# A two-layer graph kernel: the gate with tokens stationary and 256 weight columns moving, c brought to tokens through DRAM, one pool of eight PSUM banks, every order from a table

## The chip, the cores and the metric

The kernel runs on one core of a Trainium2 chip. The metric is the time of one execution on the device, in microseconds. A core has five engines with a queue of instructions each: TensorE (PE, matmuls into PSUM), VectorE (DVE), ScalarE (ACT), GpSimd (POOL) and SyncE (SP), which here issues all DMAs. An instruction starts when those ahead of it on its engine have started and the semaphores that it waits for have been reached, so the order on each engine is part of the kernel. PSUM has eight banks of 128 x 512 fp32.

## The reference

64 graphs of N = 256 tokens with H = 512 features, all fp32, and an adjacency `adj` of 256 x 256 per graph. Cut to what is computed:

```python
h = relu(layernorm(x))
q, k, v = h @ Wq.T, h @ Wk.T, h @ Wv.T               # 8 heads of 64
s = where(adj != 0, q @ k.T / 8, -inf)               # per head
c = softmax(s) @ v
gate = sigmoid(concat([c, h]) @ Wg.T + bg)
x = x + gate * h + (1 - gate) * c
h = relu(layernorm(x))
wh = h @ W
e = leaky_relu(wh @ a1 + (wh @ a2).T, 0.2)
x = x + elu(softmax(where(adj == 0, -1e9, e)) @ wh)
```

## The kernel before

Per graph there are four large products, q and k together, v, the gate's z and wh, each of 256 tokens by 512 by 512 (z by 1024). They use a Strassen-like scheme of seven products of halves (`strassen`, L163). The products 1, 2, 3 and so on accumulate in three PSUM banks a, b and c (matmuls at L179); ACT copies bank a out (L192: u1 and quadrant c00) and DVE adds banks b and c to earlier sums (L190: u2, u3, c11, c10, c01). Sums of the weights are made once on DVE; sums of the tokens' operand for every product on POOL (`token_sums`, L157 to L160; tile S).

Layer 0. x is loaded, normalised (bn on DVE L201 to L205, power on POOL L209, relu on ACT L218), transposed as 32 x 32 blocks on DVE (L261) and completed by a trip through DRAM: four sends, four fetches (`send_blocks`, `fetch_blocks`). hT then is channel-major. Scores (L360) of the eight heads take 16 matmuls in two halves; DVE finds each row's maximum with the mask (L375), ACT takes exp with its sum (L384), DVE the reciprocal (L392), POOL (three quarters, L399) or ACT scales, DVE transposes blocks (L408), and the attention weights go through DRAM to become eT (one send and four fetches a quarter). `a_weigh` (L440) multiplies them with v into pc, which ACT copies to cT, channel-major (L450).

The gate, `g_gate`, uses `on_channels` (L316): a 128 x 128 block of the weight is stationary and 128 token columns move, so that z is channel-major. tanh (L483) takes bg per channel as its bias. POOL makes d = hT - cT (L478); DVE makes d = (z + 1) d (mix 1, L491) and z = d / 2 + cT (mix 2, L493), which is y, transposes its blocks (L509), and y comes to tokens through DRAM (`g_send`, `g_fetch`); `g_residual` (L531) adds it to x on DVE. The last two graphs transpose y on PE (L504).

Layer 1 normalises x again and brings h1 through DRAM; wh has two extra columns, from which come the logits (pe, a transpose on PE, L586). The softmax's weights eg go through DRAM to egT. `g_out` (L645) has four matmuls of 512 columns a graph into two banks po. DVE takes neg = min(po r, 0) (L658), ACT pos = relu(po r) (L663) and exp of neg (L664), DVE adds (elu, L669), POOL adds to x (L674), and x is stored.

PSUM: banks ma, mb and mc serve the products and two or three of the scores, pool w with five banks all else. `emit_round(i)` (L698) writes out the order of all engines for one round by hand: PE does pc, scores, po, z, wh, qk with pe in it, and v, of four graphs at different stages (p = i + 1, q = i - 1, r = i - 2, o = i - 3). `emit_end` writes out the last rounds. Graphs below FIRST = 3 and from LAST = 62 on are transposed on PE.

Of the kernel before, what the change touches and what calls it, by code (L numbers as in the profile page):

```python
# [20 lines left out]

@with_exitstack
def kernel(
# [13 lines left out]

# [9 lines left out]
    FIRST, LAST = 3, B - 2  # L65
    assert N == 256 and H == 512 and SCALE == 0.125

    def pool(name, bufs, **kw):
# [3 lines left out]
    st = pool("st", 3)  # L72
    sb = {tag: pool(tag, bufs) for tag, bufs in {
        "x": 5, "adj": 1, "mask": 4, "hT": 3, "S": 3, "qk": 2, "v": 2, "wh": 1, "e": 5,
        "cT": 1, "z": 2, "h": 1, "tmp": 5, "U": 3,
    }.items()}
    ps = {tag: pool(f"ps_{tag}", bufs, space=bass.MemoryType.PSUM) for tag, bufs in {
        "ma": 1, "mb": 1, "mc": 1, "w": 5,
    }.items()}
    dram = pool("dram", 4, space=bass.MemoryType.DRAM)  # L80

# [3 lines left out]
    nc.gpsimd.memset(mhalf, -0.5)  # L85

    graphs = {}

    def load_graph(g):
        xt = sb["x"].tile([P, NT, H], F32, tag="t", name=f"x_{g}")  # L90
        at = sb["adj"].tile([P, NT, N], I32, tag="t", name=f"adj_{g}")
        for ts in [slice(0, NT)] if g > 0 else [slice(t, t + 1) for t in range(NT)]:
            nc.sync.dma_start(xt[:, ts, :], x[g].rearrange("(t p) h -> p t h", p=P)[:, ts, :])
        graphs[g] = {"x": xt, "adj": at}
        if g > 0:
            load_edges(g)

    def load_edges(g):
        nc.sync.dma_start(graphs[g]["adj"], adj[g].rearrange("(t p) n -> p t n", p=P))
# [4 lines left out]
    def load_weight(key, eng):  # L104
        w = weight[key] = const.tile([P, HC, 2, HH + (key == "1")], F32, name=f"w{key}_sb")
        for n in range(2):
            eng.dma_start(w[:, :, n, :HH], sources[key][:, n * HH:(n + 1) * HH].rearrange("(c p) f -> p c f", p=P))

    def weight_sums(key):

        w = weight[key]
        t = const.tile([P, 3, 2, w.shape[3]], F32, name=f"w{key}_t")
        b11, b12, b21, b22 = (w[:, r:r + 2, n, :] for r in (0, 2) for n in range(2))
        weight[key] = {1: b11, 2: b21, 3: b22, 4: t[:, 2], 5: b12, 6: t[:, 0], 7: t[:, 1]}
        return [lambda args=args: nc.vector.tensor_tensor(*args) for args in (
            (t[:, 1], b22, b12, ALU.subtract),
            (t[:, 0], t[:, 1], b11, ALU.add),
            (b12, b12, b11, ALU.subtract),
            (t[:, 2], b21, t[:, 0], ALU.subtract),
        )]  # L120

    a_sb = [sb["tmp"].tile([P, H], F32, tag="t", name=f"a_sb_{side}") for side in range(2)]
    hbg = const.tile([P, HC], F32, name="hbg")

    def load_small():
        for side in range(2):
            nc.sync.dma_start(a_sb[side], bass.AP(tensor=a.tensor, offset=a.offset + side * H, ap=[[0, P], [1, H]]))
        with nc.allow_non_contiguous_dma(reason="512 biases, once"):
            nc.sync.dma_start(hbg, bg.rearrange("(c p) -> p c", p=P))

    def edge_columns():

        w = weight["1"]

        def column(c, side):
            scr = sb["tmp"].tile([P, 2, HH], F32, tag="t", name=f"scr_{c}_{side}")
            nc.vector.scalar_tensor_tensor(
                scr, w[:, c, :, :HH], 1.0, a_sb[side].rearrange("p (n f) -> p n f", n=2),
                ALU.mult, ALU.mult, accum_out=w[:, c, side, HH:],
            )  # L140

        return [lambda c=c, side=side: column(c, side) for c in range(HC) for side in range(2)]

    def evac(dst, src, on_act):
        if on_act:
            nc.scalar.copy(dst, src)
        else:
            nc.vector.tensor_copy(dst, src)


    def token_sums(hT, name):

        s = sb["S"].tile([P, 4, 2, P], F32, tag="t", name=f"S_{name}")
        a11, a21 = hT[:, 0, 0:2, :], hT[:, 1, 0:2, :]
        a12, a22 = hT[:, 0, 2:4, :], hT[:, 1, 2:4, :]
        eng = nc.gpsimd
        eng.tensor_tensor(s[:, 0], a21, a22, ALU.add)  # L157
        eng.tensor_tensor(s[:, 1], s[:, 0], a11, ALU.subtract)
        eng.tensor_tensor(s[:, 2], a11, a21, ALU.subtract)
        eng.tensor_tensor(s[:, 3], a12, s[:, 1], ALU.subtract)  # L160
        return {1: a11, 2: a12, 3: s[:, 3], 4: a22, 5: s[:, 0], 6: s[:, 1], 7: s[:, 2]}

    def strassen(name, shape, mms, dst):  # L163

        bank, u = {}, {}
        where = {"1": "a", "2": "a", "6": "b", "7": "b", "4": "b", "5": "c", "3": "c"}
        sums = {"u2": ("b", "u1"), "u3": ("b", "u1"), "c11": ("c", "u3"), "c10": ("b", "u1"), "c01": ("c", "u2")}  # L170

        def run(step):
            if step in where:
                key, first, last = where[step], step in "165", step in "243"
                if first:
                    bank[key] = ps[f"m{key}"].tile(shape, F32, tag="t", name=f"pm{key}_{name}")
                todo = mms(int(step))
                for i, (cols, lhsT, rhs) in enumerate(todo):
                    nc.tensor.matmul(  # L179
                        bank[key][(slice(None), *cols)], lhsT, rhs,  # L180
                        start=first and i == 0, stop=last and i == len(todo) - 1, skip_group_check=True,
                    )
                return
            if step[0] == "u":
                out = u[step] = sb["U"].tile(shape, F32, tag="t", name=f"{step}_{name}")
            else:
                out = dst[int(step[1])][int(step[2])]
            if step in sums:
                key, other = sums[step]
                nc.vector.tensor_tensor(out, bank[key], u[other], ALU.add)  # L190
            else:
                nc.scalar.copy(out, bank["a"])  # L192

        return run

    def norm_stats(s, t, name):

        if t == 0:
            s["mv"] = st.tile([P, NT, 2], F32, tag="mv", name=f"mv_{name}")
        bs = st.tile([P, 6], F32, tag="bs", name=f"bs_{name}_{t}")  # L200
        nc.vector.bn_stats(bs, s["x"][:, t, :])  # L201
        nc.vector.bn_aggr(s["mv"][:, t, :], bs)
        if t == NT - 1:
            s["ve"] = st.tile([P, NT], F32, tag="ve", name=f"ve_{name}")
            nc.vector.tensor_scalar_add(s["ve"], s["mv"][:, :, 1], EPS)  # L205

    def norm_root(s, name):
        s["rs"] = st.tile([P, NT], F32, tag="rs", name=f"rs_{name}")
        nc.gpsimd.tensor_tensor(s["rs"], s["ve"], mhalf, ALU.pow)  # L209

    def norm_bias(s, name):
        s["nb"] = st.tile([P, NT], F32, tag="nb", name=f"nb_{name}")
        nc.vector.scalar_tensor_tensor(s["nb"], s["mv"][:, :, 0], -1.0, s["rs"], ALU.mult, ALU.mult)  # L213

    def norm_relu(s, name):
        h = sb["h"].tile([P, NT, H], F32, tag="t", name=f"h_{name}")
        for t in range(NT):
            nc.scalar.activation(  # L218
                h[:, t, :], s["x"][:, t, :], AF.Relu, bias=s["nb"][:, t:t + 1], scale=s["rs"][:, t:t + 1]
            )  # L220
        return h


    def p_mask(g):
        s = graphs[g]
        s["mask"] = sb["mask"].tile([P, NT, N], BF16, tag="t", name=f"mask_{g}")
        nc.vector.tensor_scalar(s["mask"], s["adj"], 0.0, MASKED, ALU.is_equal, ALU.mult)

    def p_stats(g, t):
        norm_stats(graphs[g], t, f"l0_{g}")  # L230

    def p_root(g):
        norm_root(graphs[g], f"l0_{g}")

    def p_bias(g):
        norm_bias(graphs[g], f"l0_{g}")

    def p_norm(g):
        graphs[g]["h"] = norm_relu(graphs[g], f"l0_{g}")

    def p_first():

        s = graphs[0]
        s["h"] = sb["h"].tile([P, NT, H], F32, tag="t", name="h_l0_0")
        mv, ve, rs, nb = (
            st.tile([P, NT, n], F32, tag=tag, name=f"{tag}_l0_0") for tag, n in (("mv", 2), ("ve", 1), ("rs", 1), ("nb", 1))
        )
        for t in range(NT):
            bs = st.tile([P, 6], F32, tag="bs", name=f"bs_l0_0_{t}")
# [4 lines left out]
        for t in range(NT):  # L254
            nc.vector.scalar_tensor_tensor(nb[:, t, :], mv[:, t, :1], -1.0, rs[:, t, :], ALU.mult, ALU.mult)
            nc.scalar.activation(s["h"][:, t, :], s["x"][:, t, :], AF.Relu, bias=nb[:, t, :], scale=rs[:, t, :])
# [790 lines left out]
```

## Time and profile before

| | us |
|---|---|
| three runs | 3148.56 to 3149.49, median 3148.71 |
| profiled execution, span from first to last instruction | 3150.9 |
| first matmul of qk, graphs 0, 1 and 2 | 9.2, 39.5, 88.0 |
| first matmul of po of the last graph | 3140.2 |

The profiled execution's own time is not listed beside its span; the span lies 2.2 us above the median of the runs. The granted clock is 0.999 in the mean. Queue 1 moved 585 MB in 1.1 million packets and took 74.8% of the 16 DMA engines. In profile rows a group such as `pmb_z<-S_c,wgc_t` names the output and the inputs as tiles; times are in us, the mean of one instruction in ns, and behind the second bar stand the idle time before the group and what ended it.

### The profile page before, as it was taken

What the parts mean: (1) busy time and instruction counts of PE and PEld (TensorE: products, weight loads), DVE (VectorE), ACT (ScalarE), POOL (GpSimd) and SP (SyncE); (2) the same over time, 40 slices, a digit from 0 to 9 for tenths busy, and PEclk for the clock granted to TensorE, in tenths of its full rate; (3) what the DMA queues carried; (4) which work ended last, traced back from release to release, by engine and by line L of the source; (5) the groups of instructions that cost most, each with busy time, mean ns of one, the idle gap of its engine ahead of it and who ended that gap; (6) DMA issues with size and microseconds to landing.
All of it is one profiled execution on the core that took longest, in us unless ns stands there. A gap on an engine that the chain in (4) does not pass through costs nothing.

```text
span 3150.9 us, 66781 instructions
## 1 busy us (share of the span) xinstructions
PE 3118.2 (99%) x22768; PEld 2726.6 (87%) x22768; DVE 2486.6 (79%) x6373; ACT 1419.0 (45%) x3977; POOL 1524.0 (48%) x2178
## 2 busy tenths in 40 slices
PE   8999999999999999999999999999999999999998
PEld 7888988888889889888888888888988988889886
DVE  7787787877877877878778778787787787877876
ACT  3354453453544544435435445354454453543543
POOL 3354454544544545545445455454454554544543
PEclk9999999999999999999999999999999999999999
DMA  5777878778777777787787777877878778778772
GB/s 171 188 184 182 202 182 196 194 184 203 185 182 203 188 192 196 179 205 188 178 210 183 188 189 183 203 186 181 206 185 194 192 181 205 187 179 209 184 178 81
DMA packets 1098180, 589.60 MB, mean 187 GB/s; under 512 B 681584, under 2 KB 1024112, under 8 KB 1097840
## 3 DMA queue, kind: packets, MB, share of 16 engines
q1 hardware_dynamic: 1097840, 585.32, 74.8%
q8 instruction: 183, 3.00, 0.4%
q14 instruction: 157, 1.29, 0.1%
HBM read 304.35 MB, written 280.76 MB: 186 GB/s over the span
## 4 chain that ended last, share of the span: by engine, by line
PE 94%; DVE 2%; DMA 2%; SPq 1%; ACT 0%; issue 0%; POOL 0%; DVEq 0%; ACTq 0%
PE pmb_z L179 11%; PE pmb_qk L179 10%; PE pma_z L179 7%; PE po L645 7%; PE pmc_z L179 7%; PE ps L360 7%; PE pma_qk L179 7%; PE pmc_qk L179 7%; PE pc L440 7%; PE pmb_wh L179 5%; PE pmb_v L179 5%; PE pmc_wh L179 3%; PE pma_wh L179 3%; PE pmc_v L179 3%; PE pma_v L179 3%; DMA eT<-there_e 1%
## 5 line engine op out<-in xcount | busy, mean ns | idle before, releaser
L384 ACT ACTIVATE e<-e,low 128x256 f32<-128x256 f32 x1024 | 508.3, 502 | 65.8 <-DVE low L375 64.9
L209 POOL TENSOR_TENSOR rs_l<-ve_l,mhalf 128x2 f32<-128x2 f32 x127 | 88.5, 697 | 882.3 <-DVE ve_l L205 882.3
L375 DVE CUSTOM_DVE_ANT_0 e<-ps,mask 128x256 f32<-128x256 f32 x1024 | 362.1, 415 | 102.7 <-PE ps L360 102.7
L399 POOL TENSOR_SCALAR e<-e,rec 128x256 f32<-128x256 f32 x768 | 354.6, 480 | 149.9 <-DVE rec L392 101.8
L408 DVE STREAM_TRANSPOSE eb<-e 128x512 f32<-128x512 f32 x512 | 351.6, 696 | 78.5 <-POOL e L399 65.4
L674 POOL TENSOR_TENSOR x<-x,pos 128x512 f32<-128x512 f32 x122 | 152.7, 1273 | 285.7 <-DVE pos L669 285.7
L218 ACT ACTIVATE h_l<-x,nb_l,rs_l 128x512 f32<-128x512 f32 x254 | 193.1, 808 | 214.9 <-DVE nb_l L213 134.8
L440 PE MATMUL pc<-eT,v 128*64 128x256 f32 x2048 | 239.5, 384 | 7.7 <-DMA eT<-there_e 6.9
L360 PE MATMUL ps<-qk 64*128 64x256 f32 x2048 | 239.0, 383 | 0.9 <-DVE qk L190 0.9
L645 PE MATMUL po<-wh,egT 128*128 128x512 f32 x512 | 237.0, 605 | 0.7 <-ACT egT L628 0.7
L360 PEld LDWEIGHTS ps<-qk 64*128 64x128 f32 x2048 | 193.4, 187 | 45.2 <-DVE ve_l L205 20.0
L157 POOL TENSOR_TENSOR S_l<-hT_l 128x256 f32<-128x256 f32 x128 | 95.6, 747 | 275.0 <-DMA hT_l<-there_h 242.6
L440 PEld LDWEIGHTS pc<-eT,v 128*64 128x64 f32 x2048 | 141.9, 137 | 97.2 <-issue 17.6
L261 DVE STREAM_TRANSPOSE h_l<-h_l 128x512 f32<-128x512 f32 x246 | 166.6, 696 | 54.8 <-ACT h_l L218 54.8
L384 ACT ACTIVATION_READ_ACCUMULATOR e<-e,low 128x1 f32 x1024 | 197.6, 193 | 0.0
L645 PEld LDWEIGHTS po<-wh,egT 128*128 128x128 f32 x512 | 92.2, 190 | 113.2 <-issue 92.0
L201 DVE BATCH_NORM_STATS2 bs_l<-x 128x6 f32<-128x512 f32 x254 | 171.6, 676 | 0.1
L483 ACT ACTIVATE z<-z,hbg 128x256 f32<-128x256 f32 x256 | 116.5, 504 | 105.8 <-DVE z L190 105.8
L450 ACT COPY cT<-pc 128x512 f32<-128x512 f32 x128 | 74.9, 586 | 190.7 <-PE pc L440 190.7
L478 POOL TENSOR_TENSOR d<-hT_l,cT 128x512 f32<-128x512 f32 x128 | 160.7, 1275 | 0.0
L179 PEld LDWEIGHTS pma_z<-hT_l,wgh_sb 128*128 128x128 f32 x1024 | 130.0, 193 | 29.6 <-issue 29.6
L192 ACT COPY qk<-pma_qk 128x512 f32<-128x512 f32 x64 | 37.5, 586 | 236.2 <-PE pma_qk L179 236.2
(157 smaller groups left out, 8115.6 us busy)
## 6 DMA issues: line engine op xcount, KB each, us to landing
there_e<-eb SPq DMA_DIRECT2D x256, 512.0 KB, 4.0
eT<-there_e SPq DMA_DIRECT2D x1024, 128.0 KB, 4.1
there_h<-h_l SPq DMA_DIRECT2D x492, 128.0 KB, 3.3
hT_l<-there_h SPq DMA_DIRECT2D x492, 128.0 KB, 3.2
x<-in_x_dram SPq DMA_DIRECT2D x63, 512.0 KB, 3.9
out_dram<-x SPq DMA_DIRECT2D x63, 512.0 KB, 4.6
there_y<-y SPq DMA_DIRECT2D x62, 512.0 KB, 3.0
yT<-there_y SPq DMA_DIRECT2D x248, 128.0 KB, 3.7
```

Of the source, the lines that this page charges most:

```text
L179: nc.tensor.matmul(bank[key][(slice(None), *cols)], lhsT, rhs, start=first and i == 0, stop=last and i == len(todo) - 1, skip_group_check= ...
L201: nc.vector.bn_stats(bs, s["x"][:, t, :])
L218: nc.scalar.activation(h[:, t, :], s["x"][:, t, :], AF.Relu, bias=s["nb"][:, t:t + 1], scale=s["rs"][:, t:t + 1])
L261: nc.vector.transpose(h[:, t, :], h[:, t, :])
L360: nc.tensor.matmul(psc[jj, i][:, t, :], qk[r:r + DK, 0, jj, t * P:(t + 1) * P], qk[r:r + DK, 1, jj, :], start=True, stop=True,)
L375: nc.vector.tensor_tensor_reduce(s["e", half, jj][:, i, t, :], s["ps", half][jj, i][:, t, :], s["mask"][:, t, :], -SCALE, HUGE, ALU.add, A ...
L384: nc.scalar.activation(e, e, AF.Exp, bias=s["low", half][:, jj, i, t:t + 1], scale=-1.0, accum_out=s["sums", half][:, jj, i, t:t + 1],)
L399: nc.gpsimd.tensor_scalar(e, e, rec[:, i, t:t + 1], 1.0, ALU.mult, ALU.mult)
L408: nc.vector.transpose(s["eb", half, jj][:, :, 4 * i:4 * i + 4, :].rearrange("p b n c -> p n b c"), e)
L440: nc.tensor.matmul(pc[i * DK:(i + 1) * DK, jj, :].rearrange("p (t a c) -> p t a c", t=NT, c=32), s["v"][:, kc, hd * DK:(hd + 1) * DK], eT[ ...
L478: nc.gpsimd.tensor_tensor(d, s["hT"][:, :, js, :], s["cT"][:, :, js, :], ALU.subtract)
L645: nc.tensor.matmul(pm, s["egT"][:, t, kc, :], s["wh"][kc][:, :, :HH], start=(kc == 0), stop=(kc == NT - 1))
```

## The change

The kernel is rewritten as named steps. A table (`PLAN`) gives each step of a graph a key; graph g's keys are shifted by 48 g, and the instructions of all engines are written in the order of the sorted keys. The keys order the work and hold no instruction back. Graphs 0, 1, 2, 61, 62 and 63 have tables of their own (`MOVED`), the weights and what is done once another. What changes in the work:

- z is computed with tokens stationary and 256 weight columns moving, as v and wh already were. z comes out by tokens. The bias now lies along the columns: DVE adds it where it takes c00 out of bank a (L383, was a copy on ACT), and POOL adds it to u2, c10 and c11 (`biasing`, L390: three instructions of 128 x 256).
- c itself is transposed by blocks on DVE (`tc_`, L644) and goes through DRAM (`send_c`, `fetch_c`), y no longer does. h is made a second time, by tokens, on ACT (`again`, two of 128 x 512). POOL makes d - c (`diff`) and x + c (`plus`), two of 128 x 512 each. DVE makes (z + 1) d (`mix`) and then x = d / 2 + x (`res`), which takes the place of mix 2 and of the addition of y.
- po has eight matmuls of 256 columns a graph (L802) instead of four of 512.
- All PSUM tiles come from one pool of eight banks. adj lies in the pool tmp; x has 4 buffers (was 5), mask 3 (was 4), h 2 (was 1). FIRST = 2, and LAST = 62 holds for egT too (was LAST - 1).
- Every exp, scaling, transpose and total is a step of its own. Steps are named product.part (`qk.u1`, `wh.c10`), `max.hji` and `exp.hji` for half h, pair j, head i, `we` for the matmuls of pc, `po.t`, `neg.t`, `pos.t`, `xn.t` (exp of neg), `elu.t`, `add.t` for the row block t.

In the built order, PE of a steady round does the following: wh's and z's groups in turn with pe among them, the rest of z, qk with v.1 in it (qk.6 to qk.4), po.1, po.0, v.6, qk.3, sc.0 (eight score matmuls), pc, sc.1 (the other eight), and the rest of v, mixed with the first of wh. DVE around this place: neg.1, qk.c10, elu.1, neg.0, v.u2, elu.0, max.000, max.001, rec.00, qk.c01, max.010, turn.001, max.011. ACT: pos.1, xn.1, pos.0, v.u1, xn.0, the four exps of 000 and 001. SP issues 52 DMAs a round, as before, in the order there_c, adj, c, there_e 00, there_h, eT 00, hT, there_g, there_e 10, 01 and 11, egT, eT 01, 11 and 10, there_h1, out, h1T, x.

The core of the diff (the table of a steady graph is cut to its parts around the scores, the gate and po):

```diff
-    FIRST, LAST = 3, B - 2
+    FIRST, LAST = 2, B - 2
...
-        "x": 5, "adj": 1, "mask": 4, "hT": 3, "S": 3, "qk": 2, "v": 2, "wh": 1, "e": 5,
-        "cT": 1, "z": 2, "h": 1, "tmp": 5, "U": 3,
+        "x": 4, "mask": 3, "hT": 3, "S": 3, "qk": 2, "v": 2, "wh": 1, "e": 5,
+        "cT": 1, "z": 2, "h": 2, "tmp": 5, "U": 3,
...
-    ps = {tag: pool(f"ps_{tag}", bufs, space=bass.MemoryType.PSUM) for tag, bufs in {
-        "ma": 1, "mb": 1, "mc": 1, "w": 5,
-    }.items()}
+    ps = pool("ps", 8, space=bass.MemoryType.PSUM)
...
+qk.c11@7.713 qk.4@8.038 qk.c10@8.845 v.6@9.888 qk.3@10.508 sc.0@12.5 v.u1@13.047 v.u2@13.932 max.000@14.256
+max.001@14.568 exp.000@15.12 exp.001@15.307 rec.00@16.501 scale.001@16.56 qk.c01@17.137 max.010@17.753
+turn.001@18.015 max.011@18.139 scale.000@18.256 sc.1@18.495 v.7@18.547 v.5@19.32 v.2@19.814 max.101@19.887
...
+fetch.10@63.663 we.01@64.269 we.10@64.517 we.11@65.623 cT.1@65.931 cT.0@67.935 tc.0@68.178 tc.1@68.862
+z.1@70.621 Sg.1@71.204 again.0@71.805 Sc.0@72.846 sc_c@73.436 again.1@74.487 Sc.1@76.35 fc@76.652 z.6@77.432
+Sc.3@77.753 Sg.3@79.038 z.u1@80.986 Sc.2@81.017 z.u2@83.459 plus.0@83.493 z.5@83.895 z.7@84.755 plus.1@85.174
+diff.1@85.992 z.u3@87.161 z.c11@88.054 z.u2b@88.325 z.2@89.486 z.c00@89.717 z.c11b@89.726 z.3@89.799 z.4@90.441
+tanh.11@90.924 z.c01@91.769 tanh.01@95.639 z.c10@96.01 z.c10b@97.905 tanh.10@98.145 mix.1@98.236 res.1@98.964
+diff.0@99.559 tanh.00@99.951 mix.0@100.406 st1.1@100.781 res.0@100.798 st1.0@100.966 root1@101.973 nb1@102.977
...
+sg@139.411 fg@148.441 po.1@152.197 po.0@152.604 pos.1@152.634 neg.1@152.713 xn.1@153.592 elu.1@153.6
+neg.0@154.07 pos.0@156.444 xn.0@157.095 add.1@157.968 elu.0@158.19 add.0@158.822 store.1@161.344 store.0@161.344
...
-            f"z_{g}", [P, 2, P], on_channels([(weight["gh"], s["hS"]), (weight["gc"], s["cS"])]), dst
+    product("z", [P, HH], on_tokens(("gh", "Sg"), ("gc", "Sc")), quadrant("z"), biased=True)
...
+            elif biased and what == "c00":
+                nc.vector.tensor_tensor(out, s[name, "a"], bias[:, 0, :], ALU.add)
...
+        def biasing(g, what):
+            s = graphs[g]
+            part = s[name, "u2"] if what == "u2" else dst(s, g, 1, int(what[2]))
+            nc.gpsimd.tensor_tensor(part, part, bias[:, int(what != "c10"), :], ALU.add)
...
-            nc.gpsimd.tensor_tensor(d, s["hT"][:, :, js, :], s["cT"][:, :, js, :], ALU.subtract)
+    @step("again.0", "again.1")
+    def again(s, g, t):
+        s["d", t] = new("tmp", [P, H], f"d_{g}_{t}")
+        relu(s, s["d", t], t, 0)
...
+        d = by_blocks(s["d", t])
+        nc.gpsimd.tensor_tensor(d, d, s["c"][t], ALU.subtract)
...
+        xt = by_blocks(s["x"][:, t, :])
+        nc.gpsimd.tensor_tensor(xt, xt, s["c"][t], ALU.add)
...
-            nc.vector.scalar_tensor_tensor(d, z, 1.0, d, ALU.add, ALU.mult)
-            nc.vector.scalar_tensor_tensor(z, d, 0.5, s["cT"][:, :, js, :], ALU.mult, ALU.add)
+        nc.vector.scalar_tensor_tensor(s["d", t], s["z"][:, t, :], 1.0, s["d", t], ALU.add, ALU.mult)
+        nc.vector.scalar_tensor_tensor(s["x"][:, t, :], s["d", t], 0.5, s["x"][:, t, :], ALU.mult, ALU.add)
...
-                pm, s["egT"][:, t, kc, :], s["wh"][kc][:, :, :HH], start=(kc == 0), stop=(kc == NT - 1)
+                    po[:, n, :], s["egT"][:, t, kc, :], to_wh(s, g, kc, n)[:, :HH],
+                    start=(kc, n) == (0, 0), stop=(kc, n) == (NT - 1, 1), skip_group_check=True,
...
+        for _, name, g in sorted(events, key=lambda e: e[0]):
+            once[name]() if g is None else steps[name](g)
```

## The prediction

> **What bounds the kernel now.** I read the busy shares first, then the chain of work that ended last, then the stretches of the run, then the timeline of TensorE (PE) in one steady round.
>
> ```profile
> PE 3118.2 (99%) x22768; PEld 2726.6 (87%) x22768; DVE 2486.6 (79%) x6373; ACT 1419.0 (45%) x3977; POOL 1524.0 (48%) x2178
> ...
> PE 94%; DVE 2%; DMA 2%; SPq 1%; ACT 0%; issue 0%; POOL 0%; DVEq 0%; ACTq 0%
> ```
>
> PE is busy for 99% of the span and is 94% of the chain: the time is PE's work plus its few waits. The stretches tell where those are. Columns: stretch, its length, then busy time (instructions) of PE, PEld, DVE, ACT and POOL, granted clock, DMA share, GB/s.
>
> ```profile
> 0.00:50.00 50.00, 42.68 (x326) 40.00 (x327) 33.32 (x88) 17.36 (x48) 14.57 (x30) 1.00 0.58 190
> 50.00:100.00 50.00, 45.66 (x340) 40.23 (x339) 37.05 (x102) 17.82 (x53) 17.06 (x27) 0.93 0.60 165
> 100.00:150.00 50.00, 47.04 (x355) 41.65 (x354) 37.69 (x99) 19.82 (x58) 20.92 (x32) 1.00 0.75 180
> 150.00:3030.00 2880.00, 2876.29 (x21054) 2517.81 (x21053) 2296.00 (x5907) 1317.79 (x3703) 1423.54 (x2028) 1.00 0.77 190
> ```
>
> Of the 2880 us in the middle PE lacks 3.7; of the first 150 it lacks 14.6, with the clock at 0.93 in the second row. So the middle can only gain from less PE work, and loses whatever new wait the change puts on PE; the head can gain waits.
>
> A steady round is 48.30 us long (the first qk matmul starts at 1007.62, 1055.92 and 1104.21). Its pieces, from the starts of groups on PE's timeline:
>
> ```profile
> 1026.48 3.67 PE L440 MATMUL pc<-eT,v 128*64 128x256 f32 x32
> 1030.08 3.72 PE L360 MATMUL ps<-qk 64*128 64x256 f32 x32
> 1033.74 3.71 PE L645 MATMUL po<-wh,egT 128*128 128x512 f32 x8
> 1037.28 0.94 PE L179 MATMUL pma_z<-hT_l,wgh_sb 128*128 128x128 f32 x7
> ```
>
> pc 3.60, scores 3.66, po 3.54; then z 12.51 (to 1049.79), wh 6.13 (to 1055.92), qk 12.50, pe about 0.2 and v 6.04. The timeline keeps two records for an fp32 matmul; the distance from one to the next is 0.1116 us at 128 columns, 0.2158 at 256 and 0.4425 at 512.
>
> **z and po.** z drops from 56 matmuls of 128 columns to 28 of 256: from 112 x 0.1116 = 12.50 to 56 x 0.2158 = 12.08, **-0.42** a round. po goes from 8 records of 512 to 16 of 256: 3.54 to 16 x 0.2158 = 3.45, **-0.09**. Over 64 graphs: -0.51 x 64 = -32.6 us. Bounds: 0 (no gain from width) and -0.51. I take the whole, since wh and v already run in the new z's form (tokens stationary, 256 or 257 columns moving) at that spacing.
>
> The Trainium skill ("TensorE: Matmul & The Clock Gate", section "Wait — 56ns, not 53.3ns?") gives every warm matmul a fixed cost of about 2.5 ns beside its columns. By that rule the 56 records fewer of z would save 0.14 us a round and po's 8 records more would lose 0.02, some -8 us in all instead of -32.6, and the forecast would be some 25 us higher. The rows above say 0.41, and rows decide.
>
> **Other engines, a round.** POOL gains three bias additions of 128x256 (as S_g, 0.73) and two plus of 128x512 (as the residual addition L674, 1.27): +4.7, to 28.5 of 48. ACT gains two again (L218, 0.81 each) and loses the copy of c00: +1.2, to 24. DVE loses mix 2 (2 x 0.81) and the addition of y (2 x 0.69), gains res (2 x 0.69 to 0.81) and c00 (0.42): about -1. All stay below PE, so volume costs nothing; only an order can. c's trip through DRAM (1 + 4 DMAs) takes the place of y's, so SP issues 52 DMAs a round as before. c is wanted only by diff and plus, z's work later (12 us of PE and more), against about 11 us for the two turns (0.64 each), the send (3.0 to land) and four fetches (3.7, issued over 2 to 3): hidden. If its cover went, mix.1 and then qk.u3 would be late.
>
> **The wait that I expect.** In before the four DVE and ACT steps on po lie beside z, and the 16 score matmuls run in one piece behind pc:
>
> ```profile
> L663 ACT ACTIVATE pos<-po,rec 128x512 f32<-128x512 f32 x128 | 87.4, 683 | 56.4 <-DVE neg L658 56.3
> L664 ACT ACTIVATE neg<-neg 128x512 f32<-128x512 f32 x128 | 79.8, 624 | 0.0
> ```
> ```profile
> L669 DVE SCALAR_TENSOR_TENSOR pos<-neg,pos 128x512 f32<-128x512 f32 x126 | 117.0, 928 | 1.6 <-ACT neg L664 1.6
> L658 DVE TENSOR_SCALAR neg<-po,rec 128x512 f32<-128x512 f32 x128 | 90.9, 711 | 0.3 <-PE po L645 0.2
> L375 DVE CUSTOM_DVE_ANT_0 e<-ps,mask 128x256 f32<-128x256 f32 x1024 | 362.1, 415 | 102.7 <-PE ps L360 102.7
> ```
>
> In the new order po runs beside v and qk, and the same steps stand directly ahead of the maxima that free the score banks. neg and pos of one po read one bank, and the second waits for the first (the 56.3 us of the L663 row). I walk from the end of po.1 = 0. Steps: 0.20 from PE to DVE or ACT, 0.04 between these two, 0.10 from DVE to POOL, 0.11 from DVE to PE, and on one engine the next start lies 0.64 (512 wide) or 0.34 (a maximum) after the last, all from the timeline. ACT pos.1 0.20 to 0.89; DVE neg.1 0.93 to 1.64; qk.c10 to 2.26; ACT xn.1 1.68 to 2.30; DVE elu.1 from 2.34, neg.0 2.99 to 3.70; ACT pos.0 3.74 to 4.43, v.u1 from 4.33, xn.0 4.58 to 5.20; DVE elu.0 5.24, four maxima from 5.89 to 7.26; four exps from 6.36 (0.47 behind the first maximum, 0.495 each) to 8.44; DVE rec.00 waits for the fourth, 8.48; qk.c01 8.57; max.010 9.18; turn.001 9.87 (its POOL scaling is done at about 9.7); max.011 10.51 to 11.28. The last bank of the second score half waits for max.011: PE may go on at 11.39. PE's own work over the stretch: po.0 1.73, v.6 0.86, qk.3 1.79, first score half 1.83, pc 3.60, four matmuls of the second half 0.92 and one record 0.11, sum 10.84. **PE waits 0.55 us in every round**, and what is queued behind is its whole order. Bounds: 0.2 if each of some ten hand-overs is 0.03 shorter, 0.9 if one elu runs at its mean of 928 ns and not at the 683 of its undisturbed ones. Times 61 rounds: +33.6 (12 to 55). It eats the saving almost to the microsecond.
>
> The rest of the round: qk.4 waits for u3, which stands on DVE behind mix.1, res, mix.0, statistics and the mask; mix.1 waits for tanh.10 and this for the last bias on POOL. By the same steps there is about 0.5 us to spare, so 0, bounds 0 and +0.55. The wait of pc for fetched eT is listed with 6.9 us in 8 times, of which 2.6 fall in the head and 1.6 in the tail; pc now runs later behind its fetches: -3, bounds -3 and 0.
>
> L669 and its like decide both places: DVE additions of two SBUF operands have a median of 683 ns and a longest of 1225, and the long ones stand beside POOL's TENSOR_TENSOR (one of 1.21 at 1043.01, beside S_l). The Trainium skill ("SBUF — State Buffer", section "SBUF: two separate sides") calls the port pair of VectorE and GpSimd an exclusive lock: a DVE instruction with two SBUF inputs and a GpSimd one that reads SBUF block each other whole. It speaks against this change, which adds five such POOL instructions; were each of the five to delay one DVE step by the 0.54 seen, and all of it on the path, a round would pay 2.7 us and the total some 165. I don't take it: DVE has six such steps of 512 columns a round where it had eight.
>
> **Ends.** From the first qk(0) at 9.23 to qk(2) at 88.02 are 78.8 us; PE's instructions between them, at the spacings above, are 64.1. 14.7 are waits and slow clock. New orders for graphs 0 to 2 put v and score halves into these gaps. Bounds: -14.7 (all gone) and +6.7 (graph 0 waits in full for c, 3.0 + 3.7); I take half of the gap, **-7**. In the tail PE loses 16 transposes of y, but wh(62) no longer covers the DVE steps of z(63): 0, bounds -4 and +4.
>
> **Sum.** On the profiled 3150.9: -32.6 + 33.6 - 3 - 7 = -9, 3142. The runs' median lies 2.2 below the span: **3140**.
>
> **Rivals.**
> A, PE stays full: the walk is too slow by 0.55, a twentieth of it. For it: the wait is a small difference of two long sums, and the two elu may start at once behind xn; against it: POOL's scaling leaves turn.001 only 0.1 to spare. 3150.9 - 32.6 - 3 - 7 - 2.2 = **3106**. Chance 0.25.
> B, the forecast, 3140; with the wait's and the head's bounds 3118 to 3160. Chance 0.43.
> C, slower: a second wait a round, at qk.4, because POOL's new additions stretch mix.1 or res from 685 to 1184 ns (the longest of L493) ahead of u3 on DVE. For it: those rows; against it: the two fewer DVE steps. Price up to 0.55 a round x 61 = +33.6 on B: **3173**. It ends above before from 0.15 us a round on (9 us / 61). Chance 0.24.
> D, a fetch comes late: SP runs one list, and a send waiting for its turn holds the fetches behind it. Over 1 us a round, **3200 or more**; the slack that I find for hT, h1T, egT and eT is 2 to 5 us, so 0.08.
>
> A measurement of this kernel tells about 0.2% (6.3 us) from no change: faster is below 3142.4, slower above 3155.0. A gives 0.25 faster; B 0.23 faster, 0.14 same, 0.06 slower; C 0.03 same, 0.21 slower; D slower. Faster 0.48, same 0.17, slower 0.35. The range goes from A's lower edge, 3100, to C's, 3178, and leaves out D and the ends of A and C.
>
> **What would show it.** z's records 0.216 apart and a round's PE work near 47.8. In the waits of PE: "ps <- DVE low" near 0.55 x 61 = 33 us (right), near none (A), or pmb_qk <- DVE u3 of tens of us (C), or a DMA row of over 60 (D). qk(2) between 75 and 88 us after the start. The step that I trust least is the walk.

## The result and the profile after

| | before | after |
|---|---|---|
| 20 runs each, side by side | 3146.89 to 3150.88, median 3148.76 | 3152.50 to 3157.05, median 3154.93 |
| ratio to before | | 1.0019, 95% interval 1.0012 to 1.0026 |
| a second set, 21 and 11 runs | median 3152.07 | median 3153.62, ratio 1.0002, interval 0.9993 to 1.0011 |
| span of the profiled execution | 3150.9 | 3153.3 (its own time 3155.37) |

The changed kernel is as fast as before or some 0.2% slower. 3140 was forecast, 9 us faster. The page of the changed kernel, busy shares and chain:

```profile
PE 3123.9 (99%) x19668; PEld 2729.8 (87%) x19668; DVE 2435.7 (77%) x6310; ACT 1471.4 (47%) x4039; POOL 1836.1 (58%) x2502
...
PE 95%; DMA 1%; DVE 1%; SPq 1%; POOL 1%; issue 0%; ACT 0%; DVEq 0%; POOLq 0%; ACTq 0%
```

PE is as full as before, although z has less work. The page shows where the work went: the score matmuls are busy for 279.9 us, in before for 239.0 (the second row).

```profile
L565 PE MATMUL ps<-qk 64*128 64x256 f32 x2048 | 279.9, 392 | 0.4 <-DVE low L575 0.4
L360 PE MATMUL ps<-qk 64*128 64x256 f32 x2048 | 239.0, 383 | 0.9 <-DVE qk L190 0.9
```

Only 0.4 us of idle time is put down to the score matmuls: a wait in the middle of a group of matmuls hides in the modelled end of the one before. It has to be read from starts. PE's timeline of one steady round, start and duration:

```profile
1010.38 3.63 PE L802 MATMUL po<-wh,egT 128*128 128x256 f32 x16
1013.85 1.03 PE L368 MATMUL pmb_v<-wv_t,Sh 128*128 128x256 f32 x4
1014.71 1.05 PE L368 MATMUL pmc_qk<-Sh,wq_sb 128*128 128x128 f32 x8
1015.60 1.06 PE L368 MATMUL pmc_qk<-Sh,wk_sb 128*128 128x128 f32 x8
1016.59 2.00 PE L565 MATMUL ps<-qk 64*128 64x256 f32 x16
1018.51 3.67 PE L625 MATMUL pc<-eT,v 128*64 128x256 f32 x32
1022.12 2.41 PE L565 MATMUL ps<-qk 64*128 64x256 f32 x16
1024.46 1.13 PE L368 MATMUL pmb_v<-wv_t,Sh 128*128 128x256 f32 x4
```

The first score half takes 1.92 from start to start, the second 2.34. Such differences, summed by kind over a round:

| us a round | qk | v | pc | scores | po | z | wh | pe | sum |
|---|---|---|---|---|---|---|---|---|---|
| before | 12.50 | 6.14 | 3.60 | 3.66 | 3.54 | 12.50 | 6.13 | 0.22 | 48.30 |
| after | 12.59 | 6.15 | 3.60 | 4.27 | 3.47 | 12.09 | 6.08 | 0.21 | 48.46 |

z, po and wh give 0.54; the scores take back 0.61 and qk, whose last group stands ahead of the first half, 0.09. But the 0.07 of po and the 0.09 of qk are not what they seem. Where PE goes from 128 x 128 blocks of the stationary operand to the smaller blocks of pc (128 x 64) and of the scores (64 x 128), or back, the groups at that place take some 0.1 longer. In PE's timeline of before:

```profile
1507.86 1.03 PE L179 MATMUL pmb_v<-wv_t,hT_l 128*128 128x256 f32 x4
1508.72 1.03 PE L179 MATMUL pmc_v<-wv_sb,S_l 128*128 128x256 f32 x4
1509.68 3.67 PE L440 MATMUL pc<-eT,v 128*64 128x256 f32 x32
...
3135.12 3.60 PE L645 MATMUL po<-wh,egT 128*128 128x512 f32 x8
3138.56 0.89 PE L626 MATMUL ptr<-ident,eg 128*128 128x128 f32 x4
```

The last group of v ahead of pc takes 0.96 and the one before it 0.86. And po of graph 62, which stands behind 128 x 128 matmuls and not behind the scores, takes 3.44 (3135.12 to 3138.56) where it takes 3.54 in a steady round. So 8 records of 512 columns cost no more than 16 of 256 (3.44 and 3.47), and po gains nothing by its new form. In the changed kernel the 0.1 behind the scores stands on v (1024.46 to 1025.43 above, 0.97), and the 0.09 that v paid ahead of pc is paid by qk ahead of the scores.

And along the span, cut at the starts of qk of graphs 3 and 62:

| us | to qk(3) | 59 rounds | from qk(62) on |
|---|---|---|---|
| before | 137.0 | 2855.8 | 158.1 |
| after | 127.1 | 2858.5 | 167.7 |

The head gives 9.9, the middle takes 2.7, the tail 9.6. (The middle of before has 59 rounds of 48.30 and 6 us of waits, most of them of pc for eT, which the changed kernel no longer has.) In the profile of the second set the changed kernel has 124.4, 2858.9 and 167.7: the head's gain is sure to some 3 us, the middle and the tail come out again.

### The profile page after: what moved, and what is told of

Its sections match the earlier page's. It is cut to its first block, busy times and chain, and to the rows that moved or that the text cites. A ratio compares the mean times of both kernels' runs of the same rounds, so it can differ in the third digit from the quotient of the medians.

```text
span 3153.3 us, 61657 instructions
## 1 busy us (share of the span) xinstructions
PE 3123.9 (99%) x19668; PEld 2729.8 (87%) x19668; DVE 2435.7 (77%) x6310; ACT 1471.4 (47%) x4039; POOL 1836.1 (58%) x2502
## 4 chain that ended last, share of the span: by engine, by line
PE 95%; DMA 1%; DVE 1%; SPq 1%; POOL 1%; issue 0%; ACT 0%; DVEq 0%; POOLq 0%; ACTq 0%
PE pmb_qk L368 10%; PE pmb_z L368 10%; PE ps L565 8%; PE pma_qk L368 7%; PE pmc_qk L368 7%; PE pc L625 7%; PE pma_z L368 7%; PE po L802 7%; PE pmc_z L368 7%; PE pmb_v L368 5%; PE pmb_wh L368 5%; PE pma_wh L368 3%; PE pmc_wh L368 3%; PE pma_v L368 3%; PE pmc_v L368 3%; PE pe L746 0%
## 5 line engine op out<-in xcount | busy, mean ns | idle before, releaser
L436 ACT ACTIVATE h<-x,nb_l,rs_l 128x512 f32<-128x512 f32 x256 | 195.0, 808 | 292.7 <-DVE nb_l L431 266.3
L565 PE MATMUL ps<-qk 64*128 64x256 f32 x2048 | 279.9, 392 | 0.4 <-DVE low L575 0.4
L426 POOL TENSOR_TENSOR rs_l<-ve_l,mhalf 128x2 f32<-128x2 f32 (+1 forms) x129 | 90.6, 702 | 297.1 <-DVE ve_l L422 269.2
L802 PE MATMUL po<-wh,egT 128*128 128x256 f32 x1024 | 237.3, 384 | 3.2 <-ACT egT L784 2.9
L802 PEld LDWEIGHTS po<-wh,egT 128*128 128x128 f32 x1024 | 192.5, 193 | 29.8 <-ACT egT L784 3.5
L352 POOL TENSOR_TENSOR S<-h1T 128x256 f32<-128x256 f32 x128 | 93.7, 732 | 202.9 <-DMA h1T<-there_h 126.9
L816 DVE TENSOR_SCALAR neg<-po,rec 128x512 f32<-128x512 f32 x128 | 95.7, 748 | 132.5 <-ACT pos L822 129.6
L768 ACT ACTIVATE eg<-eg,nm 128x256 f32<-128x256 f32 x128 | 64.0, 500 | 274.3 <-DVE nm L762 274.3
L822 ACT ACTIVATE pos<-po,rec 128x512 f32<-128x512 f32 x128 | 88.0, 687 | 210.6 <-issue 118.1
L444 DVE STREAM_TRANSPOSE h<-h 128x512 f32<-128x512 f32 x248 | 172.0, 701 | 8.7 <-ACT h L436 3.3
L673 POOL TENSOR_TENSOR d<-d,c 128x512 f32<-128x512 f32 x128 | 164.4, 1285 | 0.0
```

Of the source, the lines that this page charges most:

```text
L436: nc.scalar.activation(out, s["x"][:, t, :], AF.Relu, bias=s["nb", layer][:, t:t + 1], scale=s["rs", layer][:, t:t + 1])
L444: nc.vector.transpose(h, h)
L565: nc.tensor.matmul(s["ps", half, jj, i][:, t, :], qk[r:r + DK, 0, jj, t * P:(t + 1) * P], qk[r:r + DK, 1, jj, :], start=True, stop=True,)
L673: nc.gpsimd.tensor_tensor(d, d, s["c"][t], ALU.subtract)
L802: nc.tensor.matmul(po[:, n, :], s["egT"][:, t, kc, :], to_wh(s, g, kc, n)[:, :HH], start=(kc, n) == (0, 0), stop=(kc, n) == (NT - 1, 1), s ...
```

## The experiments

The theory after the result: the second score half waits for max.011 on DVE, as in the walk; cutting the scores has a price of its own; and the tail has lost its cover. The rival for the round: what is longer is not a wait but only the price of the cut, or the wait hangs on POOL. Ratios are to before on the same chip.

**turn.001 behind max.011.**

```diff
-turn.001@18.015
+turn.001@18.2
```

> The changed kernel with one step moved on DVE: turn.001 behind max.011 and not ahead of it. In the changed kernel's steady round (48.46 us between equal points of PE) the second score half takes 2.34 us where it takes 1.93 in the head. Theory (the walk of the prediction): the bank of the last matmuls is freed by max.011, which comes 0.64 earlier now, so the 0.41 goes: a round of 48.05, and 59 rounds x 0.41 = -24 us, some 3130. Rival (the 0.41 is the price of matmuls of another row height behind pc, or another bank is late next): the second half stays above 2.2 us and the time within 5 us of 3155.

Measured: 3130.64 beside 3152.51, ratio 0.9930 (0.9915 to 0.9945). PE's timeline:

```profile
1534.21 2.00 PE L565 MATMUL ps<-qk 64*128 64x256 f32 x16
1536.14 3.67 PE L625 MATMUL pc<-eT,v 128*64 128x256 f32 x32
1539.74 2.00 PE L565 MATMUL ps<-qk 64*128 64x256 f32 x16
1541.67 1.13 PE L368 MATMUL pmb_v<-wv_t,Sh 128*128 128x256 f32 x4
```

The second half now takes 1.93 (1539.74 to 1541.67), a round 48.05. The wait is settled, and this version beats both kernels. A second set, beside the changed kernel itself:

> turn.001 behind max.011, once more, beside the changed kernel. Theory: 59 rounds x 0.41 shorter than the changed kernel, -24 us and some 3 us in the head, ratio to before 0.992 to 0.994. Rival: none of the earlier difference was of the round; then the ratio would be that of the changed kernel.

Measured: 3133.36, ratio 0.9935 (0.9923 to 0.9947), where the unaltered kernel, run for this comparison,

> The changed kernel itself, beside the next three on the same chip, since the ratio to before is needed to 0.1% (the kernel before was measured at 3148.8 in one set of runs and 3151 to 3153 in two others). Theory (the two kernels' difference holds): ratio 1.001 to 1.003. Rival (0.2% is within what changes from one set to another): a ratio whose interval holds 1.

gave 3153.62 and 1.0002 (0.9993 to 1.0011): 20 us between the two. In the profiles the 59 rounds take 2836.8 instead of 2858.5, 21.7 less. So the sign of the change itself is not certain beyond 0.1%, that of the moved turn is.

**max.010 twice.**

```diff
-        for t in range(NT):
+        for t in [0, 1, 0, 1] if (half, jj, i) == (0, 1, 0) and 3 <= g < B - 3 else range(NT):
```

> The changed kernel with max.010 done twice over in the steady graphs (0.69 us more on DVE ahead of max.011, same result). Theory (the second score half waits for what DVE does ahead of max.011, microsecond for microsecond): the second half takes 2.34 + 0.69 = 3.03 us, a round 49.15, 58 rounds x 0.69 = +40 us on the changed kernel, some 3195. Rival (the wait is for something else that the turn merely disturbs, such as POOL's scaling): the second half stays at 2.3 to 2.5 and the time within 8 us of the changed kernel.

Measured: 3193.17, 39.6 us above the changed kernel in the same set; a round of 49.15. Now the profile shows the wait too:

```profile
1525.61 1.56 PE L565 MATMUL ps<-qk 64*128 64x256 f32 x10
1527.58 1.13 PE L565 MATMUL ps<-qk 64*128 64x256 f32 x6 [0.41 <-DVE low L575]
1528.63 1.13 PE L368 MATMUL pmb_v<-wv_t,Sh 128*128 128x256 f32 x4
```

3.02 for the half. The wait follows DVE's work ahead of max.011 microsecond for microsecond; the rival falls.

**The cut in the kernel before.** `a_scores(p, 0)` ahead of `a_weigh(i, 0)`, `a_scores(p, 1)` behind `a_evac(i, 1)`.

> The kernel before with the scores cut in two: eight score matmuls, then pc, then the other eight; all other orders are unchanged. Theory (each change between matmuls of 128 rows and of 64 rows costs PE about 0.1 us, and the cut adds 0.2 to 0.3 a round even when no bank is waited for): score matmuls of 3.86 instead of 3.66, a round of 48.5 to 48.6, 3162 to 3168. Rival (the cut itself is free and the changed kernel's longer score matmuls are all waiting): score matmuls of 3.66, 3145 to 3152.

Measured: 3251.53, ratio 1.0316 (1.0299 to 1.0333). The total says nothing of the cut, since a new wait came ahead of the first half; the rows inside do:

```profile
1506.87 2.00 PE L360 MATMUL ps<-qk 64*128 64x256 f32 x16 [1.40 <-DVE v L190]
1508.80 3.67 PE L440 MATMUL pc<-eT,v 128*64 128x256 f32 x32
1512.40 2.00 PE L360 MATMUL ps<-qk 64*128 64x256 f32 x16
1514.33 3.71 PE L645 MATMUL po<-wh,egT 128*128 128x512 f32 x8
```

Both halves take 1.93 with no bank to wait for, 3.86 instead of 3.66 in one piece: 0.20 for the cut. The 0.09 on qk ahead of the first half in the changed kernel is no second price, since before pays the same ahead of pc. The forecast of the time missed: the first scores share a bank with v, whose last sum DVE had not done (87 us in 63 rounds).

**pc ahead of both halves in the changed kernel.** Ten keys altered: fetch.10 and we.* ahead of sc.0, cT.* ahead of the exps, qk.c01 and max.01* ahead of rec.00.

> The changed kernel with the steady graphs' table altered around the scores: pc, and the last fetch for it, ahead of both score halves, the copies of pc ahead of the exps on ACT, qk.c01 and all four maxima of half 0 ahead of rec.00. PE then does pc, sc.0 and sc.1 in one piece, and the second half's banks are those of pc and of max.000 and max.001. Theory (wait 0.41 and cut 0.20 to 0.30 are both gone): a round of 47.75 to 47.9, 3155 - 59 x 0.6 = 3118 to 3124. Rival (a new wait takes its place: pc for the fetch that now has 1.9 us less, or the banks of pc for the copies on ACT): 3140 or more, with that wait in PE's list. If only the wait goes and the cut is free: 3130.

Measured: 3263.97, ratio 1.0354 (1.0339 to 1.0369): the rival. The scores take 3.75 in one piece, but a round takes 50.39. On DVE the first maximum starts 10.98 behind the start of po (7.67 in the changed kernel), and v.3 waits 1.69 for v.c11 behind the maxima. A second attempt with v.u3 and v.c11 earlier on DVE:

> The changed kernel with pc ahead of both score halves as before (that run's round was 50.39 us, with v.3 waiting 1.7 us for v.c11 on DVE), and with v.u3 ahead of turn.001, v.c11 right behind max.101 and the two statistics of layer 0 later on DVE. Theory (the one piece of score matmuls saves 0.3 us on PE, but puts the maxima 2.9 us later on a DVE that has no such slack, and a bank or a total is then late wherever the order is changed): v.3's wait falls from 1.7 below 0.5, another wait on DVE's work comes up behind it, and the round stays above 48.3. Rival (v.c11 was the only late step): a round of 47.8 to 48.0, some 3120.

Measured: 3311.65, ratio 1.0509 (1.0495 to 1.0524). v.3 no longer waits, wh does, for DVE: 139.6 us in 57 rounds. So the cut costs 0.2 us of PE, of which one piece got back 0.11 here (3.86 to 3.75), and buys DVE a start 3.3 us earlier, which these two orders can't do without.

**z's width alone, in the kernel before.** z's matmuls with tokens stationary; what follows reads z in the wrong layout.

> The kernel before, with only z's matmuls turned: tokens stationary, 256 weight columns moving (28 of 256 for 56 of 128). Everything behind reads z as if it were channel-major, so the output is not the reference's; the amount and order of all other work is unchanged. Theory (the saving is in the shape, 0.42 us a round, and nothing else in this order takes it back): 3148.8 - 64 x 0.42 = 3122. Rival 1 (the saving per matmul is about 2.5 ns a record, 0.14 us a round): 3140. Rival 2 (the round of before is bounded by another engine or by the fetches, so that PE waits instead): 3146 to 3151.

Measured: 3145.31, ratio 0.9976 (0.9967 to 0.9985), 7 us and not 27. z takes up to 12.25 and not 12.09, wh 6.25 where it had 6.13, a round 48.15: the second b group of each, which needs bank b free from u2 on DVE, starts 0.12 to 0.16 late (in one round u2 of z ends on DVE at 1526.92, and PE goes on at 1526.97). The width is worth 0.42 only where DVE keeps up; the order of before gives 0.28 of it back.

**Less on POOL.** turn.001 moved; bias additions and plus left out.

> The changed kernel with turn.001 behind max.011, and with the bias additions and plus left out on POOL (five instructions, 4.7 us a round; c is then not added to x, so the output is not the reference's). Theory of the prediction (volume on POOL costs nothing while PE sets the round): a round of 48.05 as with turn.001 alone, the time within 3 us of it. Rival (POOL's additions stretch DVE's steps and part of the round waits for them): a round below 48.0, and mix on DVE down from 793 ns to below 720.

Measured: 3129.73, ratio 0.9929 (0.9916 to 0.9941), a round of 48.05. The group of mix, the changed kernel first, then this run:

```profile
L687 DVE SCALAR_TENSOR_TENSOR d<-z,d 128x512 f32<-128x512 f32 x128 | 101.5, 793 | 67.6 <-ACT z L683 67.6
```
```profile
L687 DVE SCALAR_TENSOR_TENSOR d<-z,d 128x512 f32<-128x512 f32 x128 | 89.6, 701 | 65.8 <-ACT z L683 65.8
```

POOL's additions do lengthen mix, by some 91 ns (792 in the run with the turn alone), and it costs nothing.

**The ends.** The tail's slow rows, in PE's timeline and in five-microsecond stretches of the changed kernel (the granted clock is the third number from the end):

```profile
3120.99 5.41 PE L802 MATMUL po<-wh,egT 128*128 128x256 f32 x16 [2.13 <-ACT egT L784]
...
3139.39 1.39 PE L782 MATMUL ptr<-ident,eg 128*128 128x128 f32 x4 [3.54 <-ACT eg L768]
3141.52 5.51 PE L802 MATMUL po<-wh,egT 128*128 128x256 f32 x16 [0.73 <-ACT egT L784]
```
```profile
3115.00:3120.00 5.00, 3.86 (x20) 3.16 (x18) 3.71 (x6) 1.00 (x3) 4.49 (x4) 1.00 0.05 17
3120.00:3125.00 5.00, 4.01 (x11) 3.20 (x12) 3.45 (x10) 1.42 (x3) 1.50 (x2) 0.66 0.00 0
3135.00:3140.00 5.00, 1.44 (x7) 0.77 (x7) 3.64 (x8) 1.09 (x4) 0.68 (x1) 0.83 0.01 2
3140.00:3145.00 5.00, 4.27 (x11) 3.24 (x12) 0.03 (x1) 0.59 (x1) 0.59 (x1) 0.50 0.28 105
```

The listed waits of PE in the tail sum to 13.7 us (7.3 in before), and behind them the clock is low: po takes 5.25 from start to start instead of 3.47. The granted clock is 0.96 in the mean of the tail, in before 0.99. Useless matmuls in the gaps:

```diff
+    fill = {("qk.1", 2): 16, ("we.00", B - 1): 8, ("th1.1", B - 2): 10, ("tg", B - 1): 18}
```

> The changed kernel with matmuls of no use (transposes of a constant into a spare PSUM bank, 0.15 us each) put into the places where PE stands still near the ends: 16 ahead of qk.1 of graph 2, 8 ahead of pc of graph 63, 10 ahead of the transposes of h1 of graph 62, 10 and 2 ahead of po of graphs 62 and 63, 18 ahead of the last edge transposes. They are shorter than the idle times (5.2, 1.8, 2.1, 2.1, 0.7, 3.5 us). Theory (part of the 9.6 us that the tail lost is slow clock behind such idle times: the po of graph 62 took 5.25 us between starts and that of 63 5.5, where 3.47 is usual, and the granted clock there is 0.50 to 0.66): these po take 3.5 again, and the whole is 3 to 7 us shorter than the changed kernel, 3148 to 3152. Rival (the clock has nothing to do with idle time, or the added matmuls only delay what waits): 3154 to 3160.

Measured: 3150.41, ratio 0.9998 (0.9990 to 1.0007); beside the two ratios of the changed kernel that is unclear. In its profile po of graph 62 is back at 3.73 busy and that of 63 at 4.69, and the tail is 166.2 instead of 167.7. That the matmuls did it is not shown: without any, po of graph 62 took 3.73 behind 2.15 us of idle time in the first profile of the moved turn, and 5.41 behind 2.14 in the second, of the same program. With the turn moved as well:

> The changed kernel with turn.001 behind max.011 and the same useless matmuls in the idle places. Theory: the two add up, 0.993 of before less 2 to 5 us: 3122 to 3128 where before is 3149. Rival (in that kernel the idle places lie otherwise, and the matmuls do nothing): as turn.001 alone, 0.993, some 3127 to 3130.

Measured: 3127.64, ratio 0.9927 (0.9915 to 0.9940); the tail is 163.7, both po are near 3.7. Against 0.9930 and 0.9935 without it no gain is shown. What the clock is worth can be read from the two profiles of the moved turn: 0.99 in the tail and 165.8 us in one, 0.96 and 168.5 in the other, 2.7 us. So, as an estimate from these two, some 3 of the tail's 9.6 us are clock that comes and goes from run to run, and some 7 would remain at the clock of before.

> turn.001 behind max.011, and the last three graphs in the order of all steady graphs instead of tables of their own. Theory (the last graphs' own order is not what costs the tail; there is no later graph's work to cover their waits, and the steady order leaves more of them bare): the tail behind the start of qk of graph 62 is 166 us or more, up to 185. Rival (the own tables are what made the tail 9.6 us longer than that of before): a tail of 156 to 163.

Measured (no own tables for the last three graphs): 3154.61, ratio 1.0003 (0.9994 to 1.0011), a tail of 188.7. The own tables save 20 us; the steady order does worse. Whether better tables exist is not shown.

> turn.001 behind max.011, and the end in another order: the whole z of graph 63 (but for product 3) ahead of wh of graph 62 on PE, and po of graph 62 behind wh of graph 63, where PE stood still 3.5 us; h1T of graph 62 lies in the pool e, since the pool z has no third buffer. Theory (the tail is longer because the changed order mixes wh of 62 into z of 63, so that the chain from z of 63 through h, wh, the edge softmax to the last po starts late and has nothing to cover it): h of graph 63 is ready some 5 us earlier, the tail behind the start of qk of graph 62 goes from 164 to 168 us down to 157 to 162, and the time to 0.9915 to 0.9925 of before. Rival (the tail is bound by the amount of work, and order only shifts the gaps): a tail of 163 or more, 0.993 to 0.994.

Measured: 3130.61, ratio 0.9933 (0.9921 to 0.9944), a tail of 165.0: the rival. The last po no longer wait long, but z of graph 63 does (1.42 for Sc on POOL, 0.58 for u2), and wh of 62 and 63 wait 2.9 for u2. The order moved the gaps and did not close them. What would close them stays open.

> As the run with z of graph 63 first, and graph 2 transposed on PE (FIRST = 3 as before the change) so that qk of graph 2 no longer waits for hT through DRAM (3.0 to 5.2 us of PE). Theory: the wait is replaced by 1.8 us of transposes; qk of graph 2 starts at 74.5 to 76 where it started at 77 to 79.4, and the time is 1 to 4 us below the other. Rival (hT's copies or the sums on POOL are late in its place): no gain.

Measured: 3128.68, ratio 0.9929 (0.9916 to 0.9942). qk of graph 2 starts at 74.7 and not 78.4, but qk(3) only 2.0 earlier; 2 us, within the interval.

## Why the prediction was wrong, point by point

- **z**, -0.42 a round: measured -0.41 (12.50 to 12.09), with 0.05 of wh on top. The rows were right here, and the 2.5 ns a matmul of the Trainium skill ("TensorE: Matmul & The Clock Gate", "Wait — 56ns, not 53.3ns?") would have given 0.14 where 0.41 was measured.
- **po, the first step that failed**, -0.09 a round: its form gives nothing (3.44 to 3.47). The prediction divided the 3.54 behind the scores by eight and took the 0.4425 for the price of 512 columns; 0.1 of the 3.54 is the change from the scores' form, which only moved to v. Its own list of pieces showed the same price in another place: with v at 6.04 it adds up to 48.18 of 48.30, and v takes 6.14 with the 0.1 ahead of pc.
- **The cut, the second**: the prediction saw that the scores "run in one piece behind pc" and put the cut at nothing. It costs 0.20 a round, 12 us in 59.
- **The wait**, 0.55 a round (bounds 0.2 to 0.9): 0.41. The walk, from the end of po.1 at 1012.1, laid beside the measured starts: elu.0 at 1017.35 walked and 1017.44 measured, max.000 at 1018.00 and 1018.05, turn.001 at 1021.98 and 1021.98, max.011 at 1022.62 and 1022.61. On DVE it was right to 0.1 us. PE came 0.19 later than walked (0.10 in the first half and 0.09 ahead of it), so that it had less to wait.
- **The round**: +0.16 where +0.04 was forecast. Against the forecast the cut is 0.20 more and po 0.12, the wait 0.14 less and wh 0.05: some 7 us in 59 rounds. Most of the cut's price only shortened the wait; with the wait gone (the moved turn) it is paid in full.
- **The wait for eT**, -3: about -6, for half of it was not in the list of waits. **The head**, -7, with about 1.5 of shape: -9.9.
- **The tail, the third and largest step that failed**: "0, bounds -4 and +4" measured +9.6, by 6.4 us more listed waits and rows that the slow clock behind them stretched by about 6 (an estimate; between the two runs of the moved turn the clock was worth 2.7), less the work that is gone. No row of the changed order was walked there, and a balance was put in its place. Which order would cover those waits stays open.
- **The way to the median**: 2.2 was taken off the span, since the profiled execution's own time was not listed. In the later sets an execution of before took 1.7 to 1.8 us more than its span, one of the changed kernel 2.1 (3155.37 and 3153.3). So the profiled execution of before was about 4 us above its median, and that of the changed kernel only 0.4: the median is 3154.93, 1.6 above the span, where 2.2 below it was forecast.
- Sum on the span: middle +3.3, head -1.4, tail +10.6 against their forecasts, less 1.1, since the wait was counted for 61 rounds and not for the 59 of the middle: 11.4, the measured 3153.3 against the 3142 forecast. The way to the median adds 3.8.
- **Rivals.** A put the price of the wait at 33.6 us; taking the wait away (moved turn) gives 20 to 28 by the ratios, and 3130 instead of A's 3106, because the cut is not free and po gains nothing. The limits that B gives, 3118 to 3160, hold the wait's bounds alone; with the head's they are 3110 to 3175. C's second wait, at qk.4, is not there, and POOL's stretching of mix is real but hidden. The lock of the Trainium skill ("SBUF — State Buffer", "SBUF: two separate sides") is not what a round pays for: five POOL instructions fewer leave it at 48.05.

## What to carry to other kernels

When PE is full, a saving of matmul time is paid out only if the engine that frees the banks keeps up: walk that chain before counting the saving, and then use the walk to move its one step that need not stand there, here a transpose behind a maximum, worth 0.7%. Count a price for every change between forms of matmul that a new order adds, don't divide a group's time by its records when a neighbour has another form, and add the pieces of a round up to see what is missing. Read waits inside a group from start to start, since the list of waits can miss them. At the ends there is no later work to cover a wait; walk them too.

## What the runs showed of the hardware

- Score matmuls of 64 rows cost PE 0.2 us a block beside their records: 3.66 for 32 records in one block and 1.93 twice in two, in both kernels. The 128 x 128 groups beside such a block, or beside pc, take some 0.1 longer as well: 0.96 instead of 0.86 for v ahead of pc, 3.54 instead of 3.44 for po behind the scores.
- 256 moving columns a record cost less than twice 128 (z: 12.09 us a round instead of 12.50), and 512 about as much as twice 256 (po: 3.44 for 8 records, 3.47 for 16).
- PE's clock fell behind idle times of 2 to 5 us: behind 5.2 us eight records of 128 columns took 1.84 instead of 0.89 (79.41 to 81.25), at a granted 0.50. The Trainium skill ("TensorE: Matmul & The Clock Gate", "What's actually happening") states half clock behind an idle window of about 3.4 us, and this row agrees. Shorter idle times can cost the clock too: in two runs of one program po took 5.41 busy behind 2.14 us of idle time and 3.73 behind 2.15.
